# Rotary sine products and a bias-and-mask sum on GpSimd, with ScalarE copying swapped half tiles, in a kernel of four attentions and four feed-forward blocks

## The chip, the cores and the metric

The kernel runs on one core of one Trainium2 chip. The metric is the device time of one execution in microseconds (us): before the change, a median of 3104.46 over three runs (3103.13 to 3104.69). A core has five instruction queues, and each one starts its instructions in a fixed order: TensorE (PE in the profile; its weight loads are shown apart as PEld), VectorE (DVE), ScalarE (ACT), GpSimd (POOL) and SyncE (SP), which here only issues transfers. TensorE writes into PSUM; every operand of GpSimd in this kernel lies in SBUF.

## The reference, cut to what matters

The input x is 8 sequences of 128 tokens of 512 numbers. Eight blocks follow one another, each adding f(layernorm(x)) to x. The two that the change touches are the first and the third attention, with 32 heads of 128 numbers each. `ctx` is a second input that gives keys and values.

```python
# first attention: a bias per head, a mask per sequence
score = jnp.einsum('bhqd,bhkd->bhqk', h_q, h_k)
score = score + position_bias[None]
score = jnp.where(m, score, -jnp.inf)
score = jax.nn.softmax(score, axis=-1)
score = jnp.where(m, score, 0.0)
attn = jnp.einsum('bhqk,bkhd->bqhd', score, h_v)

# third attention: rotary embedding; 8 key heads for 32 query heads
def _rotate_half(x):
    x1, x2 = (x[..., :x.shape[-1] // 2], x[..., x.shape[-1] // 2:])
    return jnp.concatenate([-x2, x1], axis=-1)
q = q * cos + _rotate_half(q) * sin
k = k * cos + _rotate_half(k) * sin
scores = jnp.einsum('bhqd,bhkd->bhqk', q, k) / jnp.sqrt(jnp.float32(D))
```

The other six blocks are a mixture of low-rank experts, a small attention with heads of 8 numbers, an int8 feed-forward block, a feed-forward block whose weights are rounded to a 16-value code (NF4), a fourth attention with normed queries and keys, and a block of gated experts.

## The kernel before

**Units.** A unit is one head of one half of the batch (four sequences, `hf` 0 or 1). The first attention has 64 units (`Unit0`), the third 64 (`Unit2`), and one loop in the program runs over all 128 of them. A group `g` is four heads; in the third attention the four share one key head. While the loop is at unit u, it projects the query (and the key) of unit u+3, takes scores and softmax of unit u+2, and multiplies the probabilities of unit u with its values. After the last head of a group come the four output projections (`output`, in `out_proj`, L218), for the third attention spread over the first two units of the next group.

**One unit of the first attention.** `project_k` and `project_q` (L337 to L352) project 128 features for 512 tokens into a PSUM bank (`project`, L237), and ScalarE copies them out. `score` (L361) gets the scores of four sequences into one bank (L265). VectorE adds the bias while it reads the bank (L363), adds the mask `neg0` (bf16; -3e38 where masked) to the result (L364), takes the row maximum (L256); ScalarE exponentiates (L213); VectorE divides (L259, L366, L367). The probabilities are turned by VectorE in 32 x 32 blocks (L277) and by transfers through a scratch tensor, and `weigh` multiplies them with the values (L288), copied out by ScalarE (L290).

**One unit of the third attention.** The same, without bias, and with `rope` (L651) between projection and scores: VectorE multiplies the PSUM bank by the cosines (L653), then the lower 64 rows by their sines into the upper half of a tile `r` and the reverse (L655, L656), and GpSimd adds both (L657). The table `cs` holds cosines and, beside them, sines for the rows 0 to 63 and negated sines for the rows 64 to 127. Features lie on the partitions, so the swap of halves is a move across partitions. The query is the weight operand of the scores (`lhsT=self.q`), the key the moving one. ScalarE scales the probabilities (L694).

**Buffers.** The pools have a fixed number of buffers by name. PSUM has eight banks: two for projections and outputs of this stream (`mm`), one each for turns, scores and pv, and three for the side work. Score tiles (`s`) have two buffers, shared by name with `o` of the fourth attention (L1020); `r` and the bias share two (`rot`); queries and keys have three each, `o` six (`tile_of`).

**Side work and order.** The blocks between the first and third attention of a half run beside the units of the other stage, in slots: `slot()` is called after each piece of a unit and emits what a table has for it (`short_stages`), and with it a share of the NF4 rounding on VectorE (L725, L726), which is ordered behind the last score read (`mark`) by `issue_after`. So, beside the first half of the third attention's units, the second half of the batch goes through the experts, the small attention (L502 to L563) and the int8 block. `inv_sqrt` (L157, L159), the root of every norm, runs on GpSimd, and VectorE waits for it (L183). The row gathers for the rotary tables (L641) are issued by GpSimd too. The framework orders the instructions of each engine as they become ready by its own estimate, with the program's order as priority, gives buffers, and adds the waits; the order of an engine is then fixed.

**Start.** The first norms and context loads of sequences 0 and 1 use the main stream's wide tiles `h` (two buffers) and `sq` (one), those of 2 and 3 the side stream's.

Of the kernel before, what the change touches and what calls it, by code (L numbers as in the profile page):

```python
# [11 lines left out]
F32 = mybir.dt.float32  # L12
# [6 lines left out]
ALU = mybir.AluOpType  # L19
# [4 lines left out]
P = 128  # L24
# [4 lines left out]
HALF = 4  # L29
# [33 lines left out]
def kernel(ctx: ExitStack, tc: tile.TileContext, a, out):  # L63
    nc = tc.nc
    V, S, G, T = nc.vector, nc.scalar, nc.gpsimd, nc.tensor

    def pool(name, bufs, **kw):
        return ctx.enter_context(tc.tile_pool(name=name, bufs=bufs, **kw))
# [9 lines left out]
    ap_ = pool("att", 2)  # L78
    dram = pool("scratch", 1, space=DRAM)

    class Stream:
# [27 lines left out]
        def wide(self, tag, shape=(P, 512), bufs=2):  # L109
            return self.sb.tile(list(shape), F32, tag=tag, name=tag, bufs=bufs)  # L110
# [8 lines left out]
    def weight(src, shape=(P, 512), queue=nc.sync):  # L119
        w = wtile(shape)  # L120
        queue.dma_start(w, src)
        return w

    def by_chunk(src, queue=nc.sync):

        return [weight(src[:, c, :], queue=queue) for c in range(4)]

    def of_head(src, h):

        return weight(src[:, :, h * P:(h + 1) * P], (P, DC, P))  # L130

    def along(v, n):

        return v.unsqueeze(2).to_broadcast([v.shape[0], v.shape[1], n])

    def times(v, n):

        return v.unsqueeze(1).to_broadcast([v.shape[0], n, v.shape[1]])
# [24 lines left out]
    for b in range(B):  # L163
        t = keep.tile([P, D], F32, name=f"x{b}")
# [4 lines left out]
    neg0 = keep.tile([P, B, P], BF16, name="neg0")  # L169
# [63 lines left out]
    def project(st, w, xT):  # L233

        mm = st.mm()
        for c in range(DC):
            T.matmul(mm, lhsT=w[:, c, :], rhs=xT[:, c, :], start=c == 0, stop=c == DC - 1)  # L237
        return mm

    def tile_of(name, bufs, shape=(P, 512)):  # L240
        return qkv.tile(list(shape), F32, tag=name, name=name, bufs=bufs)
# [6 lines left out]
    class Unit:  # L248
# [17 lines left out]
            return sc  # L266

        def score_tile(self):
            return ap_.tile([P, HALF, P], F32, tag="s", name="s")

        def turn(self):
            pt = p_transposed(self.st, self.p, S)
# [12 lines left out]
        def weigh(self):  # L285
            pv = self.st.pv()
            for i in range(HALF):
                T.matmul(pv[:, i, :], lhsT=self.values(i), rhs=self.pt[i], start=True, stop=True)  # L288
            o = tile_of("o", 6, (P, HALF, P))
            S.copy(o, pv)  # L290
            self.group.o.append(o)
# [5 lines left out]
    mark = [None]  # L297
# [38 lines left out]
    class Unit0(Unit):  # L336
# [8 lines left out]
        def project_q(self):  # L345
            st, g, grp = self.st, self.g, self.group
            self.q = tile_of("q", 3)
            S.copy(self.q, project(st, of_head(a["l0_wq"][g], self.h), xT0[self.hf]))
            if self.h == 0:
                self.load_values()  # L350
            if self.h == 3:
                grp.wo = by_chunk(a["l0_wo"][g])  # L352
# [6 lines left out]
            return [self.project_k, self.project_q]  # L359

        def score(self):  # L361
            s = self.score_tile()
            mark[0] = V.tensor_add(s, self.scores(self.k), times(self.group.bias[:, self.h, :], HALF))  # L363
            V.tensor_add(s, s, neg0[:, self.hf * HALF:(self.hf + 1) * HALF, :])  # L364
            self.softmax(s)
            V.tensor_mul(self.su, self.su, anyv[:, self.hf * HALF:(self.hf + 1) * HALF])  # L366
            V.tensor_mul(s, s, along(self.su, P))  # L367
# [283 lines left out]
    def rope(dst, mm, t):  # L651

        V.tensor_mul(dst, mm, t[:, 0, :])  # L653
        r = ap_.tile([P, 512], F32, tag="rot", name="rot")
        V.tensor_mul(r[0:64, :], mm[64:128, :], t[64:128, 1, :])  # L655
        V.tensor_mul(r[64:128, :], mm[0:64, :], t[0:64, 1, :])  # L656
        G.tensor_add(dst, dst, r)  # L657

    class Unit2(Unit):
        def project_k(self):  # L660
            st, g, grp = self.st, self.g, self.group
            w = grp.w = [weight(a["l2_wkv"][g][:, 2 * j:2 * j + 2, :], (P, 2, 2 * P)) for j in range(2)]
            grp.ctx = ctxT[:, :, self.hf * 512:(self.hf + 1) * 512]
            mm = st.mm()
            for c in range(DC):
                T.matmul(mm, lhsT=w[c // 2][:, c % 2, 0:P], rhs=grp.ctx[:, c, :], start=c == 0, stop=c == DC - 1)  # L666
            grp.k = tile_of("k", 3)
            rope(grp.k, mm, cs[self.hf])
# [11 lines left out]
        def project_q(self):  # L680
            self.q = tile_of("q", 3)
            rope(self.q, project(self.st, of_head(a["l2_wq"][self.g], self.h), xT2[self.hf]), cs[self.hf])
            if self.h == 3:
                self.group.wo = by_chunk(a["l2_wo"][self.g])
# [215 lines left out]
    class L3:  # L900
# [115 lines left out]
        def weigh(self, it):  # L1016
            pv = self.st.pv()
            for j in range(2):
                T.matmul(pv, lhsT=it.v[:, j, :], rhs=it.pts[j], start=j == 0, stop=j == 1)  # L1019
            it.o = ap_.tile([P, 4, P], F32, tag="s", name="o")  # L1020
            if it.blocks:
                S.copy(it.o.rearrange("p h (a j) -> p a h j", j=32), pv.rearrange("p a (h j) -> p a h j", j=32))
            else:
                S.copy(it.o, pv)
# [68 lines left out]
    with ExitStack() as early:  # L1093
        def sub_pool(name, bufs, **kw):
            return early.enter_context(tc.tile_pool(name=name, bufs=bufs, **kw))

        ps = sub_pool("ps", 1, space=PSUM)
        qkv = sub_pool("qkv", 5)
        nfp = sub_pool("nf4", 2)
        main = Stream("m", sub_pool("main", 2), ps, {"mm": ("mm", 2), "tp": ("tp", 1), "sc": ("sc", 1), "pv": ("pv", 1)})  # L1100
        side = Stream("s", sub_pool("side", 2), ps, {k: ("side", 3) for k in ("mm", "tp", "sc", "pv", "po")})


# [112 lines left out]
        for kind in (Unit0, Unit2):  # L1216
            for hf in range(2):
                for g in range(NG):
                    grp = Group()
# [69 lines left out]
    ps = ctx.enter_context(tc.tile_pool(name="ps2", bufs=1, space=PSUM))  # L1289
# [160 lines left out]
def build(arrays):  # L1450
    import concourse.bacc as bacc

    nc = bacc.Bacc("TRN2", target_bir_lowering=False, num_devices=1)
    aps = {
        n: nc.dram_tensor(f"in_{n}", v.shape, mybir.dt.from_np(v.dtype), kind="ExternalInput").ap()
        for n, v in arrays.items()
    }
    out = nc.dram_tensor("out_0", (B, P, D), F32, kind="ExternalOutput").ap()
    with tile.TileContext(nc) as tc:
        kernel(tc, aps, out)  # L1460
    return nc
# [9 lines left out]
```

## Time and profile before

| what | value |
|---|---|
| runs | 3103.13, 3104.46, 3104.69 us |
| profiled execution: its own time / the span from its first to its last instruction | 3106.4 / 3104.6 us |
| granted TensorE clock, mean | 0.998 |
| first attention, 0 to 1103 us: busy PE / DVE / ACT / POOL | 1093.9 / 812.2 / 363.6 / 47.7 us |
| third attention, 1103 to 1893 us: busy PE / DVE / ACT / POOL | 773.5 / 647.8 / 334.3 / 127.6 us |
| NF4 feed-forward, 1893 to 2133 us: busy PE / DVE / ACT / POOL | 238.7 / 48.3 / 19.5 / 5.5 us |
| fourth attention and last block, 2133 to 3104.6 us: busy PE / DVE / ACT / POOL | 965.7 / 507.5 / 368.8 / 114.8 us |

How to read a profile here: a row of a group has the source line, the engine, the operation, the tiles it writes and reads, the shapes and the count; then the busy time in us and the mean of one in ns; then how long the engine sat idle just before and which instruction ended that. A line number can be a helper's. In the list of waits, a row is the waiting instruction, what it waited for, and total us, times and longest. In the timeline a row is start, length, engine, line, operation; the bracket is the idle time before it. The end of a matmul is modelled, and matmuls overlap one another, so that TensorE counts as busy as long as the next one starts soon enough.

### The profile page before, as it was taken

The page shows a single profiled execution, that of the slowest core. Times are in us where ns is not written, and L with a number is a line of the kernel's source. Part 1 is how long each engine was busy: PE and PEld are TensorE (multiplying, and loading weights), DVE is VectorE, ACT ScalarE, POOL GpSimd, SP SyncE. Part 2 cuts the span into 40 slices and gives each one's busy share as a digit, 9 for nine tenths or more (in the row PEclk, how much of TensorE's full clock was granted, in tenths as well). Part 3 has the DMA queues.
Part 4 walks back from the last instruction along what each step waited for, and adds up shares of the span by engine and source line. Part 5 has one row for each costly group of instructions (what it writes and reads, how often), then busy time and mean ns, then how long its engine had stood idle before and what let it go on. Part 6 is the DMA issues. An engine that isn't in the chain of part 4 may idle for free.

```text
span 3104.6 us, 34843 instructions
## 1 busy us (share of the span) xinstructions
PE 3071.9 (99%) x10976; PEld 1694.2 (55%) x10980; DVE 2015.8 (65%) x4209; ACT 1086.1 (35%) x3410; POOL 295.5 (10%) x315
## 2 busy tenths in 40 slices
PE   9999999999999999999999999999999999999999
PEld 4554555545554565555555554445665665555564
DVE  5877787667767766888989983113555555555544
ACT  3222222235543233655333332002434433333332
POOL 2000000000001021111111110001111111111110
PEclk9999999999999999999999999999999999999999
DMA  6434343333334432323444342223655655555540
GB/s 216 124 113 126 117 126 116 102 103 97 102 95 118 150 119 80 102 82 113 123 140 128 119 124 84 77 69 103 181 178 165 187 180 174 180 172 167 174 132 14
DMA packets 414807, 393.83 MB, mean 127 GB/s; under 512 B 37600, under 2 KB 312736, under 8 KB 414112
## 3 DMA queue, kind: packets, MB, share of 16 engines
q1 hardware_dynamic: 391200, 348.60, 36.6%
q10 hardware_dynamic: 23040, 41.95, 4.4%
q8 instruction: 89, 1.46, 0.2%
q0 software_dynamic: 384, 1.05, 0.1%
q14 instruction: 94, 0.77, 0.1%
HBM read 291.92 MB, written 99.55 MB: 126 GB/s over the span
## 4 chain that ended last, share of the span: by engine, by line
PE 84%; DVE 11%; ACT 2%; DMA 2%; issue 1%; POOL 0%; SPq 0%; ACTq 0%; POOLq 0%; DVEq 0%
PE mm L237 17%; PE mm L218 12%; PE po L218 7%; PE tp L921 7%; PE mm L376 7%; PE mm L944 7%; PE mm L879 5%; PE pv L1019 4%; PE sc L996 3%; PE pv L288 2%; PE mm L888 2%; PE sc L265 2%; ACT s L213 1%; DVE dq L726 1%; DVE rot L656 1%; PE mm L666 1%
## 5 line engine op out<-in xcount | busy, mean ns | idle before, releaser
L237 PE MATMUL mm<-xT,w 128*128 128x512 f32 x1024 | 464.4, 595 | 2.1 <-DVE rot L656 2.1
L218 PE MATMUL mm<-w,o 128*128 128x512 f32 x1024 | 464.0, 597 | 1.6 <-ACT o L290 1.5
L726 DVE TENSOR_TENSOR dq<-dq,ind 128x512 f32<-128x512 f32 (+2 forms) x476 | 326.8, 687 | 9.8
L237 PEld LDWEIGHTS mm<-xT,w 128*128 128x128 f32 x1024 | 188.9, 190 | 218.6 <-issue 208.6
L218 PEld LDWEIGHTS mm<-w,o 128*128 128x128 f32 x1024 | 188.5, 191 | 214.3 <-issue 199.9
L213 ACT ACTIVATE s<-s,nm 128x128 f32<-128x128 f32 x512 | 199.0, 390 | 190.2 <-DVE nm L256 179.1
L944 PE MATMUL mm<-w,xT 128*128 128x512 f32 x512 | 233.9, 592 | 0.0
L218 PE MATMUL po<-w,o 128*128 128x512 f32 x512 | 233.2, 594 | 0.0
L237 PE MATMUL mm<-ctxT,w 128*128 128x512 f32 x512 | 230.7, 593 | 1.1 <-ACT ctxT L1235 0.8
L376 PE MATMUL mm<-w,ctxT 128*128 128x512 f32 x512 | 230.4, 593 | 0.0
L725 DVE TENSOR_SCALAR ind<-nw 128x512 f32<-128x512 f32 (+2 forms) x476 | 210.5, 442 | 5.8
L213 ACT ACTIVATE p<-sc,nm,rq 128x256 f32<-128x256 f32 x256 | 141.1, 562 | 113.6 <-DVE nm L1001 109.9
L159 POOL TENSOR_TENSOR rs<-rs,mhalf 128x1 f32<-128x1 f32 x64 | 41.2, 645 | 1248.5 <-DVE rs L180 757.7
L265 PEld LDWEIGHTS sc<-k,q 128*128 128x128 f32 x1024 | 131.8, 192 | 49.5 <-issue 39.9
L219 DVE TENSOR_TENSOR x<-x,mm 128x512 f32<-128x512 f32 x128 | 87.0, 679 | 110.3 <-PE mm L218 110.0
L290 ACT COPY o<-pv 128x512 f32<-128x512 f32 x128 | 74.3, 581 | 237.6 <-PE pv L288 237.6
L218 PEld LDWEIGHTS po<-w,o 128*128 128x128 f32 x512 | 96.3, 190 | 110.6 <-issue 103.3
L879 PE MATMUL mm<-xT,w 128*128 128x512 f32 (+1 forms) x352 | 152.5, 592 | 0.8 <-DVE x L219 0.8
L376 PEld LDWEIGHTS mm<-w,ctxT 128*128 128x128 f32 x512 | 94.3, 190 | 106.2 <-issue 106.2
L1000 DVE TENSOR_REDUCE nm<-sc 128x2 f32<-128x512 f32 x128 | 85.3, 674 | 102.7 <-PE sc L996 102.5
L237 PEld LDWEIGHTS mm<-ctxT,w 128*128 128x128 f32 x512 | 93.2, 190 | 99.3 <-issue 96.8
L944 PEld LDWEIGHTS mm<-w,xT 128*128 128x128 f32 x512 | 97.0, 190 | 89.5 <-issue 84.9
(244 smaller groups left out, 4716.5 us busy)
## 6 DMA issues: line engine op xcount, KB each, us to landing
w<-in_l_wq SPq DMA_DIRECT2D x128, 256.0 KB
w<-in_l_wo SPq DMA_DIRECT2D x128, 256.0 KB
far<-tb SPq DMA_DIRECT2D x125, 256.0 KB
pt<-far SPq DMA_DIRECT2D x500, 64.0 KB
far<-tb SPq DMA_DIRECT2D x60, 512.0 KB
pt<-far SPq DMA_DIRECT2D x240, 128.0 KB
far<-tb SPq DMA_DIRECT2D x63, 384.0 KB
pt<-far SPq DMA_DIRECT2D x252, 96.0 KB
```

The source lines that it names most:

```text
L213: S.activation(dst(h), src(h), AF.Exp, bias=negm[:, h:h + 1], scale=by, accum_out=su[:, h:h + 1])
L218: T.matmul(mm, lhsT=o(h), rhs=wo[h], start=h == 0, stop=h == 3)
L237: T.matmul(mm, lhsT=w[:, c, :], rhs=xT[:, c, :], start=c == 0, stop=c == DC - 1)
L265: T.matmul(sc[:, i, :], lhsT=self.q[:, i * P:(i + 1) * P], rhs=k[:, i * P:(i + 1) * P], start=True, stop=True)
L376: T.matmul(mm, lhsT=ctxT[:, c, toks(self.hf * HALF + i)], rhs=grp.wv[c], start=c == 0, stop=c == DC - 1)
L725: V.tensor_scalar(iv, w, bound, step, cmp, ALU.mult)
L726: V.tensor_add(dst, dst, iv)
L879: T.matmul(mm[:n, :], lhsT=w[c][:, j * P:j * P + n], rhs=xT[:, c, :], start=c == 0, stop=c == DC - 1)
L921: T.matmul(it.kv[:, s, :], lhsT=lhsT, rhs=it.wkv[c // 2][:, c % 2, :], start=c == 0, stop=c == DC - 1)
L944: T.matmul(mq, lhsT=self.xT[it.hf][:, c, cols(it.b)], rhs=it.wq[c], start=c == 0, stop=c == DC - 1)
L996: T.matmul(sc[:, i, :], lhsT=it.qT[2 * j + i], rhs=it.kT, start=True, stop=True)
L1019: T.matmul(pv, lhsT=it.v[:, j, :], rhs=it.pts[j], start=j == 0, stop=j == 1)
```

## The change

In the third attention, `rope` leaves the cosine product on VectorE. ScalarE copies the two halves of the PSUM bank, swapped, into `r`; GpSimd multiplies `r` by the sine table in place, and subtracts it from the cosine product (subtracts, since each row now meets the sine of its own half, of the other sign).

In the first attention, GpSimd adds bias and mask into the score tile when the query is projected, one loop step before the scores; VectorE then makes one addition, of the scores in PSUM and that tile.

Score tiles get three buffers, and with them `o` of the fourth attention. The main stream's `h` and `sq`, used at the start, take buffers of the name "o" (six) in place of tiles of their own.

```diff
--- before.py
+++ after.py
@@ -266,7 +266,7 @@
             return sc
 
         def score_tile(self):
-            return ap_.tile([P, HALF, P], F32, tag="s", name="s")
+            return ap_.tile([P, HALF, P], F32, tag="s", name="s", bufs=3)
 
         def turn(self):
             pt = p_transposed(self.st, self.p, S)
@@ -346,6 +346,9 @@
             st, g, grp = self.st, self.g, self.group
             self.q = tile_of("q", 3)
             S.copy(self.q, project(st, of_head(a["l0_wq"][g], self.h), xT0[self.hf]))
+
+            self.masked = self.score_tile()
+            G.tensor_add(self.masked, times(grp.bias[:, self.h, :], HALF), neg0[:, self.hf * HALF:(self.hf + 1) * HALF, :])
             if self.h == 0:
                 self.load_values()
             if self.h == 3:
@@ -359,9 +362,8 @@
             return [self.project_k, self.project_q]
 
         def score(self):
-            s = self.score_tile()
-            mark[0] = V.tensor_add(s, self.scores(self.k), times(self.group.bias[:, self.h, :], HALF))
-            V.tensor_add(s, s, neg0[:, self.hf * HALF:(self.hf + 1) * HALF, :])
+            s = self.masked
+            mark[0] = V.tensor_add(s, self.scores(self.k), s)
             self.softmax(s)
             V.tensor_mul(self.su, self.su, anyv[:, self.hf * HALF:(self.hf + 1) * HALF])
             V.tensor_mul(s, s, along(self.su, P))
@@ -652,9 +654,11 @@
 
         V.tensor_mul(dst, mm, t[:, 0, :])
         r = ap_.tile([P, 512], F32, tag="rot", name="rot")
-        V.tensor_mul(r[0:64, :], mm[64:128, :], t[64:128, 1, :])
-        V.tensor_mul(r[64:128, :], mm[0:64, :], t[0:64, 1, :])
-        G.tensor_add(dst, dst, r)
+        S.copy(r[0:64, :], mm[64:128, :])
+        S.copy(r[64:128, :], mm[0:64, :])
+
+        G.tensor_mul(r, r, t[:, 1, :])
+        G.tensor_tensor(dst, dst, r, ALU.subtract)
 
     class Unit2(Unit):
         def project_k(self):
@@ -1017,7 +1021,7 @@
             pv = self.st.pv()
             for j in range(2):
                 T.matmul(pv, lhsT=it.v[:, j, :], rhs=it.pts[j], start=j == 0, stop=j == 1)
-            it.o = ap_.tile([P, 4, P], F32, tag="s", name="o")
+            it.o = ap_.tile([P, 4, P], F32, tag="s", name="o", bufs=3)
             if it.blocks:
                 S.copy(it.o.rearrange("p h (a j) -> p a h j", j=32), pv.rearrange("p a (h j) -> p a h j", j=32))
             else:
@@ -1097,7 +1101,14 @@
         ps = sub_pool("ps", 1, space=PSUM)
         qkv = sub_pool("qkv", 5)
         nfp = sub_pool("nf4", 2)
-        main = Stream("m", sub_pool("main", 2), ps, {"mm": ("mm", 2), "tp": ("tp", 1), "sc": ("sc", 1), "pv": ("pv", 1)})
+
+        class Main(Stream):
+
+
+            def wide(self, tag, shape=(P, 512), bufs=2):
+                return tile_of("o", 6, shape) if tag in ("h", "sq") else super().wide(tag, shape, bufs)
+
+        main = Main("m", sub_pool("main", 2), ps, {"mm": ("mm", 2), "tp": ("tp", 1), "sc": ("sc", 1), "pv": ("pv", 1)})
         side = Stream("s", sub_pool("side", 2), ps, {k: ("side", 3) for k in ("mm", "tp", "sc", "pv", "po")})
 
 
```

## The prediction

> **What bounds the kernel now.** The page comes first: one engine is full, and VectorE is full only in part of the span.
>
> ```profile
> span 3104.6 us, 34843 instructions
> PE 3071.9 (99%) x10976; PEld 1694.2 (55%) x10980; DVE 2015.8 (65%) x4209; ACT 1086.1 (35%) x3410; POOL 295.5 (10%) x315
> DVE  5877787667767766888989983113555555555544
> ```
>
> TensorE idles 3104.6 - 3071.9 = 32.7 us. That is all that any gain can come from. The table of busy time by stretch says where it lies (columns: stretch, length, then busy us of PE, PEld, DVE, ACT, POOL).
>
> ```profile
> 100.00:200.00 100.00, 100.00 (x329) 51.84 (x328) 83.20 (x165) 24.96 (x71) 3.12 (x4) 1.00 0.41 123
> 800.00:900.00 100.00, 100.00 (x449) 52.37 (x448) 75.63 (x146) 53.74 (x184) 1.26 (x2) 1.00 0.30 92
> 1400.00:1500.00 100.00, 95.94 (x497) 56.09 (x497) 84.49 (x165) 50.76 (x169) 17.69 (x15) 1.00 0.35 108
> 1700.00:1800.00 100.00, 99.36 (x411) 58.66 (x409) 94.40 (x166) 35.17 (x129) 15.53 (x11) 1.00 0.40 124
> ```
>
> The first attention (to 1103) has no TensorE idle time between 100 and 900, with VectorE near 80%. The third (1103 to 1893) idles 790.0 - 773.5 = 16.5 us, half of the whole; VectorE reaches 94% there. TensorE's own waits name the releasers:
>
> ```profile
> PE mm L237 <- DVE rot L656: 2.1, 6, 0.4
> ...
> PE tp L454 <- DVE hw L452: 1.9, 1, 1.9
> PE tp L596 <- DVE q L591: 1.6, 1, 1.6
> ```
>
> With the smaller ones of that stage (L521 1.0, L443 1.0, L513 0.9, L219 0.7, L534 0.6, L813 0.5), VectorE ends 2.1 + 8.2 = 10.3 us of them. L656 is the rotation's last product: it frees the PSUM bank that a projection needs.
>
> **The rows that price the change.**
>
> ```profile
> L655 DVE TENSOR_TENSOR rot<-mm,cs 64x512 f32<-64x512 f32 x80 | 55.4, 693 | 1.5
> L364 DVE TENSOR_TENSOR s<-s,neg 128x512 f32<-128x512 f32 x64 | 44.2, 690 | 0.1
> L657 POOL TENSOR_TENSOR q<-q,rot 128x512 f32<-128x512 f32 x64 | 84.9, 1326 | 416.8 <-DVE rot L656 390.7 <-PE pv L288 6.4 <-PE sc L265 6.0
> L421 ACT COPY ha<-mm 128x128 f32<-128x128 f32 x8 | 2.1, 262 | 7.0 <-DVE lg L420 7.0
> ```
>
> **First attention: nothing.** It loses 64 x 0.69 = 44 us on VectorE (L364) and gains 64 GpSimd additions. None in the trace mixes f32 with bf16; the nearest row, L657, has 1.33, and L422 1.40: about 85 us. The addition takes no input from the projection. It needs the bias, the mask and a free score tile, whose last reader is the turn of three units ago, so it can run a unit ahead. TensorE, with no idle time, hides all of it and can gain nothing. Cover gone means the scores' evacuation waiting for GpSimd; GpSimd is nearly idle here (3.1 us in 100 to 200). On its queue the additions stand ahead of the norms' powers (L159) and of the eight row gathers (L641), for whose landing TensorE waits 4.1 us near 988: one addition late there costs 1.3, one VectorE product less gains 0.7. I take 0, ends -1 and +2. At the start the mask is ready at 22.0 and the first scores come at 45.4; three additions need 4 us. The start's norm tiles in "o" and the third buffer of "s" remove waits that TensorE doesn't have (the fourth attention's "o" releases none of its waits): 0. No DMA is added or moved.
>
> **Third attention, engine time.** Removed: 80 x (0.693 + 0.684) = 110 us of VectorE. Added: 160 ScalarE copies and 80 GpSimd products. No copy of 64 rows from PSUM is in the trace; the 64-row products at 0.69 cost as much as 128-row ones, so the nearest is L290, 128x512 from PSUM, 0.58: 93 us, taking ScalarE from 334 to 427 of 790. The product is an L657, 1.27 at its shortest: 102 to 106 us.
>
> Here a rule speaks against the change. The Trainium skill, "SBUF — State Buffer", section "Who interferes with whom", says that GpSimd and a VectorE instruction with two SBUF inputs, or in a two-port mode, exclude each other, the later one blocking until the first is done. If every one of the 144 new GpSimd instructions held VectorE for its whole length, 144 x 1.3 = 187 us would be lost against 154 removed. The trace has the effect (L725 below takes 1.08 where its mean is 0.44), but smaller: summing, over the 80 rotation additions, how far VectorE instructions that overlap one exceed their group's median gives 29 us, 0.36 for each. VectorE's other work there (PSUM reads, reductions, the 32x32 turns) isn't held. By the row, the third attention loses 80 x 0.36 = 29 more: VectorE 648 - 110 + 29 = 567 of 790. By the rule it would hardly be relieved. I take the row.
>
> **Third attention, the path to the scores.** This decides. The timeline of one group of heads, near 1690, engine by engine, put in order of time:
>
> ```profile
> 1688.17 0.69 DVE L653 TENSOR_TENSOR q<-mm,cs 128x512 f32<-128x512 f32 x1 [0.84 <-PE mm L237]
> ...
> 1690.44 1.27 POOL L657 TENSOR_TENSOR q<-q,rot 128x512 f32<-128x512 f32 x1 [10.81 <-DVE rot L656]
> 1690.91 1.08 DVE L725 TENSOR_SCALAR ind<-nw 128x512 f32<-128x512 f32 x1
> ...
> 1692.77 0.19 PEld L265 LDWEIGHTS sc<-k,q 128*128 128x128 f32 x1 [0.24 <-issue]
> ...
> 1693.89 0.68 DVE L653 TENSOR_TENSOR q<-mm,cs 128x512 f32<-128x512 f32 x1
> 1694.70 1.28 ACT L694 ACTIVATE s<-s,su 128x128 f32<-128x128 f32 x4 [0.43 <-DVE su L259]
> 1695.88 0.56 ACT L290 COPY o<-pv 128x512 f32<-128x512 f32 x1
> 1696.25 1.27 POOL L657 TENSOR_TENSOR q<-q,rot 128x512 f32<-128x512 f32 x1 [4.54 <-DVE rot L656]
> ...
> 1697.99 0.19 PEld L265 LDWEIGHTS sc<-k,q 128*128 128x128 f32 x1 [0.24 <-issue]
> ```
>
> The rotated query is the weight of its scores, loaded only one projection after its own. Now the path is three products and an addition, 1688.17 to 1691.71, 1.06 before the load. After it, the cosine product and ScalarE both read the same PSUM tile; where the kernel already has that pair (L420, L421) ScalarE waits for VectorE all seven times, so I put them in a row: 0.69 + 2 x 0.58 + 2 x 1.27 = 4.39, and 0.2 for four handovers (0.04 to 0.08 each): 4.6 in place of 3.54.
>
> Second head of a group: 1688.17 + 4.6 = 1692.77, just at its load. Any 0.3 of waiting shows; I take 0.2. Third head: VectorE, with two products less ahead, can take the cosine product at about 1693.4, done 1694.1. ScalarE is then in the softmax of the head before; the score read moves from 1690.30 to about 1689.05, so the scaling L694 ends near 1694.7. Copies before the scaling: the path ends at 1698.0, in time. Behind it: copies to 1695.9, GpSimd to 1698.6, late by 0.6. Behind the copy L290 too: late by 1.6. I take 0.7, nearest the middle. (Lower end 0: at 1611.52 GpSimd ended just 0.05 before the scores' matmul and TensorE had no gap. Upper end 1.8 for both heads.) First and fourth heads have outputs between: 8.4 and 15 us to spare. So 0.9 for each group; nine groups from 1503 on: 8.1, ends 0 and 16. Before 1503 the small attention's matmuls lie between and the spare time is mostly 2 to 20 us; five early queries (1107 to 1173) have 0.1 to 1.7: 5 x 0.7 = 3.5, ends 0 and 8. **Cost 11.6.**
>
> A late load stops TensorE, hence the next projection. Behind waiting copies on ScalarE stand exponentials, scalings and the copy of pv; behind waiting products on GpSimd stand the powers of the norms, for which VectorE's L183 waits. Both delay the side work, which has slots of spare time: 0, upper end 5.
>
> **Gains.** L656's 2.1: a key's bank is freed after 0.69 + 1.16 = 1.85 instead of 2.05, and VectorE comes sooner: all of it. Of the other 8.2 most are chains of short dependent instructions, which a shorter queue helps little: a third, 3.0 (ends 0 and 8.2).
>
> **Sum** on the profiled execution: 11.6 - 2.1 - 3.0 = +6.5. That execution took 3106.4, of which 1.8 lie outside the span of 3104.6; the runs' median is 3104.46. The change is added to the median: **3111.0**. About 0.2% (6.2 us) is what a measurement of this kernel can tell from no change.
>
> **Rivals.**
> - Faster, 3097 (0.23): the instruction order puts the copies ahead of the scaling, so both paths end in time and only the gains stay, with most of VectorE's waits: -2.1 - 5.5. Place: the third head; it decides where ScalarE starts the copies within 0.1 us of the cosine product. For it: ScalarE is idle two thirds of the time there, VectorE at 94%. Against: its idle gaps beside the third head are 0.4 to 0.8 long, shorter than two copies.
> - They cancel, 3106 (0.16): lateness of 0.3 a group.
> - ScalarE's queue becomes the bound, 3128 (0.13): copies stand behind the exponentials as well, 1.8 for each group and more beside the small attention, where ScalarE has 50 to 59% already. Against: TensorE now waits under 2 us for ScalarE's exponentials and pt copies.
> - VectorE isn't relieved, 3117 (0.06): the lock takes the removed time back as the rule has it, so gains vanish and products come later.
>
> **How the numbers follow.** Forecast 0.42, of which 0.12 lies below 3110.7 and 0.30 above, own range 3107 to 3118. Faster by over 0.2%: 0.20 of the first rival. Within: 0.12 + 0.16 + 0.03 = 0.31. Slower: 0.30 + 0.13 + 0.06 = 0.49. The range, 3096 to 3128, leaves out half of the faster rival's far end and half of the ScalarE one.
>
> **What would show it.** Right: TensorE waits for GpSimd at L265, about 10 us in sum and 0.5 to 1 each, none for L656; first attention without idle time as now; VectorE about 81 us less in 1103 to 1893; ScalarE's copies at 0.58. Wrong: copies that start beside the cosine product, a GpSimd product well off 1.3 us, scores put behind other matmuls so that the load isn't late, or VectorE instructions stretched by more than 0.4 for each GpSimd one.

## The result, and the profile after

The changed kernel takes **3120.89 us** (3119.44 to 3123.88), the kernel before, run beside it, 3104.69 (3103.13 to 3108.45): a ratio of 1.005, with a 95% interval of 1.0039 to 1.006, or 16.2 us slower. 3111.0 was forecast, within a range of 3096 to 3128.

The page of the changed kernel begins as follows; the third line shows VectorE's busy share in 40 slices.

```profile
span 3119.1 us, 35219 instructions
PE 3075.0 (99%) x10976; PEld 1693.0 (54%) x10980; DVE 1925.2 (62%) x3985; ACT 1182.5 (38%) x3570; POOL 483.4 (15%) x459
DVE  5877777667766756777778873113555555555544
```

TensorE's idle time rose from 32.7 to 3119.1 - 3075.0 = 44.1 us, although VectorE has 90.6 us less to do (2015.8 - 1925.2). The busy time by stretch of the changed kernel (stretch, length, then busy us of PE, PEld, DVE, ACT, POOL, granted clock) says where:

```profile
100.00:200.00 100.00, 100.00 (x329) 51.82 (x328) 80.52 (x159) 26.06 (x74) 10.46 (x9) 1.00 0.41 123
800.00:900.00 100.00, 100.00 (x449) 52.37 (x448) 73.41 (x142) 54.50 (x187) 7.31 (x7) 1.00 0.30 92
1103.00:1893.00 790.00, 763.08 (x3357) 439.54 (x3358) 582.34 (x1035) 421.12 (x1370) 234.90 (x187) 1.00 0.37 111
1400.00:1500.00 100.00, 94.88 (x485) 54.76 (x486) 76.86 (x151) 60.65 (x187) 28.99 (x25) 0.99 0.36 116
1700.00:1800.00 100.00, 95.03 (x388) 55.37 (x388) 84.34 (x138) 48.96 (x153) 31.21 (x24) 1.00 0.37 114
```

The first attention stays full. The third has 790 - 763.08 = 26.9 us without TensorE work, where the same stretch of the kernel before has 16.5:

```profile
1103.00:1893.00 790.00, 773.54 (x3397) 447.72 (x3397) 647.80 (x1201) 334.26 (x1225) 127.63 (x107) 1.00 0.37 113
```

VectorE's relief there is 647.80 - 582.34 = 65 us. So TensorE idles more, though VectorE is less busy. The first matmuls of the groups of heads date the loss: the changed kernel is 2.4 us ahead at 1487, 3.7 behind one group later, and then loses 0.5 to 2.4 us in each, to 15 at the NF4 block. TensorE's waits in the changed kernel (us in total, times, longest):

```profile
PE sc L265 <- POOL q L661: 9.1, 10, 1.9
...
PE mm L237 <- ACT rot L658: 2.8, 6, 0.7
...
PE tp L190 <- DVE rs L180: 2.4, 1, 2.4
PE mm L670 <- DVE x L219: 2.1, 3, 1.0
```

L265 takes the scores, with the rotated query as their weight; L661 is GpSimd's subtraction, L657 and L658 are ScalarE's copies, L660 is GpSimd's product, L351 the addition of bias and mask. The changed kernel's groups of instructions (busy us, mean ns | idle time before them):

```profile
L660 POOL TENSOR_TENSOR rot<-rot,cs 128x512 f32<-128x512 f32 x80 | 106.7, 1334 | 523.9 <-ACT rot L658 511.3 <-DVE s L695 4.8 <-DVE nm L256 3.4
L351 POOL TENSOR_TENSOR s<-bias,neg 128x512 f32<-128x512 f32 x64 | 81.3, 1272 | 727.3 <-DVE tb L277 476.6 <-ACT pt L228 103.6 <-ACT v L380 51.2
...
L657 ACT COPY rot<-mm 64x512 f32<-64x512 f32 x80 | 46.6, 582 | 212.3 <-DVE q L655 146.6 <-DVE k L655 61.0 <-issue 2.5
L658 ACT COPY rot<-mm 64x512 f32<-64x512 f32 x80 | 46.2, 577 | 0.9
```

The durations are those forecast. What isn't is how VectorE fares beside GpSimd. The timeline of one third head in the changed kernel, engine by engine, put in order of time, with instructions left out in between:

```profile
1740.59 0.41 DVE L817 TENSOR_TENSOR nw<-dq,am 128x256 f32<-128x256 f32 x1
1741.19 1.27 POOL L660 TENSOR_TENSOR rot<-rot,cs 128x512 f32<-128x512 f32 x1 [9.14 <-ACT rot L658]
1741.52 1.22 DVE L817 TENSOR_TENSOR nw<-dq,am 128x256 f32<-128x256 f32 x1
1742.54 1.33 POOL L661 TENSOR_TENSOR q<-q,rot 128x512 f32<-128x512 f32 x1
1742.66 1.82 DVE L817 TENSOR_TENSOR nw<-nw,ri 128x256 f32<-128x256 f32 x2
1743.10 0.19 ACT L213 ACTIVATION_READ_ACCUMULATOR s<-s,nm 128x1 f32 x1
1744.41 0.17 DVE L259 RECIPROCAL su<-su 128x4 f32<-128x4 f32 x1
1744.60 1.28 ACT L698 ACTIVATE s<-s,su 128x128 f32<-128x128 f32 x4 [1.32 <-DVE su L259]
1745.91 0.58 ACT L657 COPY rot<-mm 64x512 f32<-64x512 f32 x1
1746.51 0.58 ACT L658 COPY rot<-mm 64x512 f32<-64x512 f32 x1
1747.16 1.51 POOL L660 TENSOR_TENSOR rot<-rot,cs 128x512 f32<-128x512 f32 x1 [3.30 <-ACT rot L658]
1748.75 1.33 POOL L661 TENSOR_TENSOR q<-q,rot 128x512 f32<-128x512 f32 x1
1750.13 1.16 PE L265 MATMUL sc<-k,q 128*128 128x128 f32 x8 [0.63 <-POOL q L661]
```

An L817 takes 0.41 us alone; beside GpSimd the same form takes 1.22, and a pair 1.82. Behind them in VectorE's queue stands the softmax's reciprocal L259, ready when the exponentials ended at 1743.29, done at 1744.58. ScalarE's scaling L698 waits for it, the copies of the next head stand behind the scaling, and TensorE waits 0.63 us at the end. Without the 1.1 us by which L259 is late, the scores would probably have been in time. This is a reading of one head; the experiments ask whether it holds for the whole.

### The profile page after: what moved, and what is told of

Its sections match the earlier page's. It is cut to its first block, busy times and chain, and to the rows that moved or that the text cites. A ratio compares the mean times of both kernels' runs of the same rounds, so it can differ in the third digit from the quotient of the medians.

```text
span 3119.1 us, 35219 instructions
## 1 busy us (share of the span) xinstructions
PE 3075.0 (99%) x10976; PEld 1693.0 (54%) x10980; DVE 1925.2 (62%) x3985; ACT 1182.5 (38%) x3570; POOL 483.4 (15%) x459
## 4 chain that ended last, share of the span: by engine, by line
PE 83%; issue 7%; DVE 4%; POOL 4%; DMA 1%; ACT 1%; SPq 0%; POOLq 0%; ACTq 0%; DVEq 0%
PE mm L237 16%; PE mm L218 10%; PE po L218 7%; PE tp L925 7%; PE mm L378 7%; PE mm L948 7%; PE mm L883 5%; PE pv L1023 4%; PE sc L1000 3%; PE sc L265 3%; PE mm L892 2%; PE pv L288 2%; POOL rot L660 2%; POOL q L661 1%; PE sc L534 1%
## 5 line engine op out<-in xcount | busy, mean ns | idle before, releaser
L730 DVE TENSOR_TENSOR dq<-dq,ind 128x512 f32<-128x512 f32 (+2 forms) x476 | 347.5, 730 | 9.8
L729 DVE TENSOR_SCALAR ind<-nw 128x512 f32<-128x512 f32 (+2 forms) x476 | 224.9, 472 | 6.1
L351 POOL TENSOR_TENSOR s<-bias,neg 128x512 f32<-128x512 f32 x64 | 81.3, 1272 | 727.3 <-DVE tb L277 476.6
L660 POOL TENSOR_TENSOR rot<-rot,cs 128x512 f32<-128x512 f32 x80 | 106.7, 1334 | 523.9 <-ACT rot L658 511.3
L265 PEld LDWEIGHTS sc<-k,q 128*128 128x128 f32 x1024 | 130.7, 192 | 60.3 <-issue 36.2
L265 PE MATMUL sc<-k,q 128*128 128x128 f32 x1024 | 138.4, 278 | 9.1 <-POOL q L661 9.1
```

What stands on the lines that cost most here:

```text
L265: T.matmul(sc[:, i, :], lhsT=self.q[:, i * P:(i + 1) * P], rhs=k[:, i * P:(i + 1) * P], start=True, stop=True)
L660: G.tensor_mul(r, r, t[:, 1, :])
L729: V.tensor_scalar(iv, w, bound, step, cmp, ALU.mult)
L730: V.tensor_add(dst, dst, iv)
```

## The experiments

**Two theories.** P is the forecast's: the path from a projection to its scores or to its free bank has become longer, and that alone costs the time. The other (L in the first expectations, H in the later ones) is that the longer path is only where it shows, and GpSimd's instructions cost the time by holding VectorE back. In what follows, "stretch" is counted from the trace as in the prediction: how far VectorE's instructions that overlap a long GpSimd instruction in the third attention exceed the median of their group, each VectorE instruction once. It is 29 us before (80 GpSimd instructions) and 73 after (160). VectorE's busy time in the stage agrees: 647.8, less the 110 of the two products, plus the 44 by which the stretch grew, is 582, and 582.34 was measured. The later expectations count an instruction that overlaps both the product and the subtraction twice (58 do), and so work with a growth of 76 us; that is too high.

**One part alone.** First the changed kernel with the old rotation, so the edits of the first attention and the buffers alone; then the kernel before with the new rotation, which is the same edit the other way round.

```diff
-        S.copy(r[0:64, :], mm[64:128, :])
-        S.copy(r[64:128, :], mm[0:64, :])
-        G.tensor_mul(r, r, t[:, 1, :])
-        G.tensor_tensor(dst, dst, r, ALU.subtract)
+        V.tensor_mul(r[0:64, :], mm[64:128, :], t[64:128, 1, :])
+        V.tensor_mul(r[64:128, :], mm[0:64, :], t[0:64, 1, :])
+        G.tensor_add(dst, dst, r)
```

> Only the first attention's part of the change (GpSimd adds bias and mask ahead; three score tiles; the start's tiles under the name o); the rotation is the one of before. Theory P (the rotated query reaches the scores' weight load too late): this part is free, 3104.7 us, within 2 either way, and TensorE has no idle time between 100 and 900 us. Theory L (GpSimd holds VectorE): at most 1 us of loss, since in the changed kernel the 64 additions stretched VectorE by 10 us in a stage where TensorE never idles. Theory F (the first attention's part is a cause): 3110 or more.

> Only the new rotation; first attention, score tiles (two) and start as before. P and L: all of the loss, 3119 to 3123 us. F: clearly less, under 3115. If the third score tile had helped the third attention, more than 3123.

The first part alone: 3103.66 us against 3104.94, ratio 0.9995 (0.9987 to 1.0004): nothing. The rotation alone: 3119.44, ratio 1.0046 (1.0032 to 1.0059): all of the loss.

**Copies ahead of the cosine product.**

```diff
-        V.tensor_mul(dst, mm, t[:, 0, :])
         r = ap_.tile([P, 512], F32, tag="rot", name="rot")
         S.copy(r[0:64, :], mm[64:128, :])
         S.copy(r[64:128, :], mm[0:64, :])
+        V.tensor_mul(dst, mm, t[:, 0, :])
```

> The changed kernel with the two ScalarE copies written ahead of VectorE's cosine product, so that the copies need not wait for it; all instructions the same in number. P: the path from projection to GpSimd's last instruction is 0.7 us shorter where ScalarE is free, TensorE's wait for GpSimd at the scores falls from 9.1 to under 4 us and the time to 3112 to 3117. L: GpSimd works as long as before, VectorE is held as much, 3119 to 3122.

3113.42 us, ratio 1.0029 (1.0018 to 1.0041): 7.5 less than after, inside P's span for the time and outside L's. TensorE's waits in this kernel:

```profile
PE sc L265 <- POOL q L660: 6.8, 10, 1.2
PE mm L237 <- DVE k L658: 6.6, 7, 1.7
```

The wait at the scores fell from 9.1 to 6.8 only, where P had under 4, and the one for the key's bank rose, since its last reader is now VectorE. The stretch fell as well, from 73 to 53 us, so the run doesn't part the two theories.

**The late scores put behind other matmuls.** The third head's scores move behind the first output projection.

```diff
-            if u + 2 < len(units):
-                units[u + 2].score()
...
+            later = isinstance(unit, Unit2) and unit.h == 0 and isinstance(units[u - 1], Unit2)
+            if not later:
+                scores()
             unit.weigh()
...
+            if later:
+                slot()
+                units[u - 1].output(0)
+                scores()
+                slot()
+                units[u - 1].output(1)
```

> The changed kernel with the third head's scores of each group written behind the first output projection of the step in place of ahead of it: 3.4 us more between that head's projection and its scores, nothing else moved by hand. P: TensorE's wait for GpSimd at the scores falls from 9.1 to 2 us or less and the time by 5 to 9 us, to 3112 to 3116. L: VectorE is held as much as in the changed kernel (GpSimd's instructions are the same), so 3119 to 3122.

3118.95 us, ratio 1.0046 (1.0033 to 1.006). Of TensorE's waits at L265 for GpSimd one of 0.3 us is left; the list begins now:

```profile
PE mm L237 <- ACT rot L658: 7.1, 6, 1.7
```

The largest wait was taken away and 2 of the 16 us came back; the rest turned up at the key's bank. The stretch stays (75 us). P in its plain form, that the late scores are the loss, falls.

**GpSimd's hold by itself.** The kernel before, with one more GpSimd product for each rotation, behind the addition, on a tile whose result nobody reads.

```diff
         G.tensor_add(dst, dst, r)
+        G.tensor_mul(r, r, t[:, 1, :])
```

> The kernel before, with one more GpSimd product behind each rotation's addition, whose result nobody reads: 80 instructions of about 1.3 us, off every path to scores, nothing taken from or added to VectorE and ScalarE. Theory H (GpSimd holds VectorE back; the lost time is side work that comes late): the stretch of VectorE instructions under GpSimd, 29 us before, grows by 0.4 to 0.9 for each of the 80, to 60 to 100 us, and the time by 6 to 16 us, to 3111 to 3121. Theory P (only the length of the path to scores and banks costs time): the path is untouched, so 3103 to 3107.

3129.59 us, ratio 1.0071 (1.0058 to 1.0085): 23 us for 80 instructions on no path, more than the whole change costs and 8 over what H expected. Its five executions lie apart, at 3123.3, 3123.9 and 3129.6 to 3130.8 us, with a granted clock of 0.995 to 0.997 where the kernel before had 0.996 to 0.998, so a part of the 23 may be the clock; the profiled one is the shortest, its span 3121.5 - 3104.6 = 16.9 us longer than before. The order of the instructions on TensorE, VectorE and ScalarE is the same as before, one by one. The stretch rose from 29 to 57 us, less than the 60 to 100 that H named. Its stage and its largest waits for VectorE:

```profile
1103.00:1893.00 790.00, 762.55 (x3345) 439.35 (x3346) 673.56 (x1195) 330.36 (x1210) 237.91 (x187) 0.99 0.36 111
```

```profile
PE mm L237 <- DVE rot L656: 3.9, 7, 1.4
...
PE mm L677 <- DVE x L219: 3.2, 5, 0.9
PE tp L454 <- DVE hw L452: 2.9, 1, 2.9
```

TensorE is idle 27.5 us in the stage, about as in the changed kernel, and no single wait stands out. Since the ends of matmuls are modelled, the waits can also be counted from their starts (how far a step from one matmul to the next exceeds the median of its form, where that is over 0.15 us): from 1096 to 1925, TensorE waits 29.4 us for VectorE where it waited 15.5 before.

The idle products could have cost time in two other ways: by holding back the powers of the norms, which stand in GpSimd's queue too, or by keeping one of the two buffers `rot` from the next rotation. Both would be waits of VectorE for GpSimd, and the only such row in the stage is, in both kernels:

```profile
DVE h L183 <- POOL rs L159: 3.3, 7, 0.7
```

**The product back on VectorE.** GpSimd keeps the subtraction alone, so it has 80 instructions as before.

```diff
-        G.tensor_mul(r, r, t[:, 1, :])
+        V.tensor_mul(r, r, t[:, 1, :])
```

> The changed kernel with the rotation's sine product on VectorE, from the copied tile in SBUF; GpSimd has the subtraction alone, as many instructions as before. VectorE still loses 80 x (1.38 - 0.7) = 54 us of products. Path: 0.69 + 2 x 0.58 + 0.70 + 1.33 + handovers = 4.1 us against 3.5 before and 4.6 to 5.6 after. Theory H: the stretch under GpSimd goes back to about 30 us, and with VectorE relieved the time falls to 3100 to 3106. Theory P: half of the added path is left, with ScalarE's copies behind the scaling: 3109 to 3114, and TensorE's wait at the scores L265 some 4 to 6 us.

3113.23 us, ratio 1.0023 (1.0013 to 1.0032): 7.7 less than after, though VectorE has 56 us more to do. P's span for the time holds, though not its 4 to 6 us at the scores; H expected a larger gain. The stretch is 35 us. The rest stands in TensorE's waits:

```profile
PE mm L237 <- ACT rot L658: 8.1, 7, 1.5
...
PE sc L265 <- POOL q L661: 3.0, 5, 1.3
```

ScalarE brings the copies late here too, and now VectorE stands in its own queue behind them: 24.7 us of idle time before the product L660.

**Some heads only.** New rotation for the first and fourth query head of a group, or for the second and third; keys and the others as before.

```diff
-            rope(self.q, project(...), cs[self.hf])
+            (rope_apart if self.h in (0, 3) else rope)(self.q, project(...), cs[self.hf])
```

> The changed rotation only for the first and fourth query head of each group, which have 8 and 15 us to spare; keys and the two middle heads as in the kernel before. Theory P: no wait for GpSimd at L265, keys' banks free as before, 3103 to 3106. Theory H: 32 of the 80 rotations have a second GpSimd instruction, so 0.4 of the 16 us is left: 3109 to 3113, and the stretch under GpSimd is some 29 + 0.4 x 76 = 60 us.

> The counterpart: the changed rotation only for the second and third query head, which have no time to spare; keys and the other two as in the kernel before. Theory P: the wait at L265 for GpSimd stays at 7 to 10 us, and the time is 3113 to 3119. Theory H: as many rotations changed as with the first and fourth head, so the same stretch (about 60 us) and 3109 to 3113.

First and fourth: 3117.83 us, ratio 1.0035 (1.0021 to 1.0049). Second and third: 3115.23, ratio 1.0027 (1.0017 to 1.0038). The heads with 8 and 15 us to spare cost at least as much as those with none. TensorE's first wait in the kernel with heads one and four:

```profile
PE mm L237 <- DVE rot L658: 9.5, 7, 1.6
```

L658 is there the last product of an old rotation, as a rule the key's. It is what it was before, where the same wait was 2.1 us; VectorE comes to it later. With heads one and four P misses by 12 us and H by 5; with two and three P's numbers hold (L265 waits 8.8 us), and H is 2 us low. Neither theory has both, and 32 rotations cost more than half of what 80 do: the cost isn't in proportion to their number.

**Copies first, and less on GpSimd.**

Against the run with the copies ahead of the cosine product, the sine product on VectorE:

```diff
-        G.tensor_mul(r, r, t[:, 1, :])
+        V.tensor_mul(r, r, t[:, 1, :])
```

> The changed kernel with ScalarE's copies ahead of the cosine product and the sine product on VectorE; GpSimd has the subtraction alone. 80 GpSimd instructions fewer than after, and both middle heads' copies no longer wait for the cosine product. Theory H (GpSimd's hold on VectorE makes most of the loss, ScalarE's late copies the rest): both causes are lessened, so 3103 to 3107, stretch under GpSimd about 30 us. Theory S (what is left of the loss with the product on VectorE, 7 us, comes from VectorE's queue standing behind copies that ScalarE brings late): the two products now both wait for the copies, so 3110 to 3115 as with the product on VectorE alone, with VectorE idle for the copies 25 us or more.

And against that, the subtraction too:

```diff
-        G.tensor_tensor(dst, dst, r, ALU.subtract)
+        V.tensor_tensor(dst, dst, r, ALU.subtract)
```

> The same, with the subtraction on VectorE too: no GpSimd instruction is left in the rotation. VectorE in 1103 to 1893 against before: 648 - 110 - 29 + 2 x 80 x 0.69 = 620 us. Theory H: no hold is left and VectorE has 28 us less than before, path 1.16 + 3 x 0.69 + handovers = 3.4 us: 3099 to 3105. Theory S: VectorE still stands behind late copies, 3108 to 3114.

With the subtraction on GpSimd 3105.27 us, ratio 0.9998 (0.999 to 1.0006), as H has it, with a stretch of 33 us; with none of the rotation on GpSimd **3093.66**, ratio 0.996 (0.9947 to 0.9974), 5 us below what H expected. S, a ScalarE queue that stays late, falls for both. Against the run with the product on VectorE and the copies behind the cosine product, the first of the two differs in the order of the copies alone: the stretch is the same (35 and 33), and 8.0 us are gone. By the starts of the matmuls, TensorE's wait for ScalarE falls there from 11.5 to 2.5 us, while the one for GpSimd rises from 4.3 to 7.8. So late copies are a cause of their own, which the hold doesn't need.

**The kernel before with its addition on VectorE.** One word differs.

```diff
-        G.tensor_add(dst, dst, r)
+        V.tensor_add(dst, dst, r)
```

> The kernel before with the rotation's addition on VectorE in place of GpSimd; nothing else. The hold of 29 us goes, 80 x 0.69 = 55 us of work comes: VectorE 648 - 29 + 55 = 674 of 790. Path to the scores 0.6 us shorter. Theory H (what counts is VectorE's time, held or worked): 26 us more of it against the 76 us that cost 16 to 22, so +3 to +8, 3108 to 3113. Theory P (length of the path): 3102 to 3106.

**3093.50 us**, ratio 0.996 (0.9946 to 0.9973): both expectations were wrong, H even in sign. A held microsecond costs more than a worked one.

**The idle product on top of that.** Path and VectorE's work as in the run just told, and again a GpSimd product for each rotation that nobody reads.

```diff
-        G.tensor_add(dst, dst, r)
+        V.tensor_add(dst, dst, r)
+        G.tensor_mul(r, r, t[:, 1, :])
```

> The kernel before with the rotation's addition on VectorE (3093.5 us) and one idle GpSimd product behind each rotation, whose result nobody reads: as many GpSimd instructions as in the kernel before, but on no path. Path to scores and VectorE's own instructions are those of the kernel at 3093.5. Theory H (each 80 long GpSimd instructions in the third attention cost 12 to 23 us, by the time they hold single VectorE instructions back): 3105 to 3116, with a stretch of 25 to 60 us. Theory P (the addition on VectorE gained by the shorter path to scores): 3091 to 3096.

3117.86 us, ratio 1.0041 (1.0027 to 1.0054): 24 us above the run without it, somewhat more than H expected and far from P. The stretch is 35 us, where the run without it has none. The two have the same order on TensorE, VectorE and ScalarE. The stage of the kernel with the addition on VectorE:

```profile
1103.00:1893.00 790.00, 780.72 (x3420) 452.26 (x3421) 669.20 (x1298) 334.56 (x1225) 22.37 (x31) 1.00 0.37 115
```

and with the idle product added to it:

```profile
1103.00:1893.00 790.00, 765.06 (x3369) 441.34 (x3369) 697.72 (x1280) 330.30 (x1210) 128.46 (x107) 1.00 0.35 111
```

The first idles 9.3 us on TensorE with VectorE busy 669, the second 24.9. By the starts of the matmuls, TensorE waits 8.5 us for VectorE in the first and 28.5 in the second. The largest of these in the second is for the score bank, which VectorE is late to read; in the first the same wait is 0.3 us:

```profile
PE sc L265 <- DVE s L692: 5.0, 6, 1.5
```

So the shorter path isn't what gained; the missing GpSimd instructions are.

The run also prices worked time. It has as many long GpSimd instructions as the kernel before (80) and nearly the same stretch (35 and 29), and VectorE has the additions besides, 80 x 0.69 = 55 us: 13.0 us more than the kernel before, beside which it ran at 3104.82. So VectorE's work isn't free either.

**All forms of the rotation side by side.** They differ in single steps, so pairs of rows price a step (the kernel before, run beside each, had medians of 3104.7 to 3106.1):

| swap of halves | sine product | sum | long GpSimd instr. | us |
|---|---|---|---|---|
| VectorE's two products | same | VectorE | 0 | 3093.50 |
| ScalarE, ahead of cosine product | VectorE | VectorE | 0 | 3093.66 |
| VectorE's two products | same | GpSimd (before) | 80 | 3104.69 |
| ScalarE, ahead | VectorE | GpSimd | 80 | 3105.27 |
| ScalarE, behind | VectorE | GpSimd | 80 | 3113.23 |
| ScalarE, ahead | GpSimd | GpSimd | 160 | 3113.42 |
| ScalarE, behind | GpSimd | GpSimd (after) | 160 | 3120.89 |

- One 128x512 operation for each rotation moved from VectorE to GpSimd: +11.2 (row 1 to 3), +11.6 (2 to 4), +8.2 (4 to 6), +7.7 (5 to 7).
- ScalarE's copies behind the cosine product and not ahead of it: +8.0 (4 to 5), +7.5 (6 to 7).
- The swap on ScalarE in place of VectorE's two products: +0.2 (1 to 2), although VectorE then has 669 - 609 = 60 us less in the stage. This is a sum of two things that no run parts, VectorE's relief and what the swap on ScalarE costs: VectorE waits 18.0 us for the copies there. Its stage in row 2:

```profile
1103.00:1893.00 790.00, 781.93 (x3439) 452.15 (x3440) 608.64 (x1218) 426.08 (x1385) 20.84 (x30) 1.00 0.37 115
```

The framework's order differs a little between the rows (in these pairs, 53 to 279 of TensorE's 10980 weight loads stand elsewhere), and the rows were not all measured beside one another, so a single pair carries some of that; that the pairs agree speaks for the step itself. Rows 2 and 4 to 7 have the first attention's edits too, which were shown to cost nothing.

## Why the prediction was right, and where it was wrong

Slower, and inside the range: 16.2 us for a forecast of 6.5. That the range held is in part luck: the largest term, late scores, turned out not to be what costs the time. From before to after the table has one product onto GpSimd (about 8), the copies behind the cosine product (about 8), and the swap on ScalarE together with VectorE's relief (0).

- **First attention, 0: right.** 3103.66 against 3104.94, no idle TensorE time from 100 to 200 and 800 to 900. VectorE loses 44 us of additions there and its busy time falls by 29 (812.2 to 783.3); some 10 of the difference are stretch under the 64 additions, about 0.15 us for each.
- **Engine time: copies and product right** (0.58 and 1.33 measured). VectorE's relief was put at 81 us and is 65, the difference being stretch.
- **The hold by the row, 0.36 us for each GpSimd instruction: the step that failed, twice.** In size: the stretch grew by 44 us where 29 was forecast, 0.55 for each new product, 0.46 for each of the 160 instructions, over the 0.4 that was named as a sign of being wrong. And in what it costs: the forecast set stretch against removed work, as if both were VectorE's time, and called the difference relief. The runs part them: 80 idle products, with a stretch of 28 and 35 us, cost 23 and 24 us of the program, 0.3 us each, while 55 us more work on VectorE beside the same number of GpSimd instructions cost 13. The rule of the Trainium skill that the forecast weighed and set aside ("SBUF — State Buffer", "Who interferes with whom": the later one waits for the whole instruction) fits by kind: beside a GpSimd instruction the changed kernel's row maxima and score reads (93 of them) took their usual time within 0.02 us on average, while the additions L730, with two inputs in SBUF, took 0.63 more. Applied to every GpSimd instruction, as the upper case of the forecast did, it overstates the stretch, 0.15 to 0.55 us measured of 1.3; but its warning was nearer to the time than the row was. Another page says as much: "Perfetto Trace Analysis", section "Optimizing Scalar/DVE Operations", notes that moving operations between these two engines might not help. Four pairs of runs here say -8 to -12 us for 80 operations moved back to VectorE.
- **Path to the scores, 4.6 us and a cost of 11.6: right in the wait, wrong in what it costs.** The wait at L265 is 9.1 in ten, 0.2 to 1.9 each, where "about 10 us" was named. The second head's path took 4.6 to 5.0, the third's mostly 5.2 to 5.6, since its copies stood behind the scaling L698, the middle case. But putting the third scores later took that wait away and gave back 1.9 us. What the order of the copies costs is 7.5 to 8.0, and where TensorE doesn't meet it at the scores, it meets it at the key's bank, which the forecast had freed sooner. Two of the five early queries waited, 2.2 us where 3.5 was put, and nothing of it is left in the time: the changed kernel is ahead at 1487.
- **Norm powers behind GpSimd's queue, 0 with an upper end of 5: one case.** At 1493.91 a norm's power became ready behind the key's L660 and L661 (1493.87 to 1496.81); L183 waited, and TensorE idled 2.4 us. That is inside the upper end.
- **Gains, 5.1: none.** L656's 2.1 became L658's 2.8: the bank is now freed by ScalarE, and both engines come late. The other waits for VectorE remained: by the starts of the matmuls, all waits for VectorE are 15.5 us before and 13.9 after, and those for ScalarE rose from 6.4 to 9.0.
- **Rivals.** The faster one had the copies ahead of the scaling decide. No run shows that order: also where they are written ahead of the cosine product, the third head's copies mostly stand behind the scaling, and that kernel still lost 8.7 us. "VectorE isn't relieved", given 0.06, named the cause of about half of the loss and put the time at 3117; its chance was too small. Its mechanism differs in one point: VectorE is relieved, in sum, and is late all the same. "ScalarE's queue becomes the bound" comes nearest to the other half, though it was the wait for the cosine product, and not exponentials ahead, that was priced.

**What stays open** is why a held microsecond costs so much more than a worked one: by the runs above 23 us of time for 28 of stretch and 24 for 35, so 0.7 to 0.8 for each (0.6 by the profiled execution of the first), against 13 for 55 of work, 0.24 (estimates, the last from a kernel whose path to the scores is also a little shorter). The 12 us that the addition on VectorE gained are then the 24 of the 80 GpSimd instructions less the price of the work. Nor does the stretch price a step by itself: the product on GpSimd adds 38 us of stretch with the copies behind the cosine product and 20 with them ahead, and costs 8 both times. The timeline shows holds in lumps of about 0.8 to 1 us, right behind a rotation, ahead of softmax steps and banks that others wait for. That the lumps are the reason is argued from it and wasn't tried.

## What to carry to other kernels

Work that is moved from VectorE to GpSimd can come back as holds of VectorE's other instructions: before moving it, add a GpSimd instruction whose result nobody reads and time that; here it cost 0.3 us of the program for each, and moving such work back was a gain that the kernel before still had, 12 us by one word. The first attention's additions, moved to GpSimd too, cost nothing, in a stage where TensorE hardly idles (1093.9 us busy of 1103). An engine's busy share says little of what its relief is worth: VectorE at 85% of the stage with hardly a GpSimd instruction beside it kept TensorE fuller than VectorE at 74% with it. And a wait that vanishes when its instruction is put elsewhere was the sign of a late engine, not the cost itself: look at what stands ahead of that engine's late instruction, and whether the time moves.

## What had not been expected of the hardware

The same GpSimd instruction form stretches VectorE very differently by what VectorE does meanwhile: about 0.15 us for each addition of the first attention, 0.36 before in the third, 0.46 for each of the 160 after, and 0.12 for the product when the cosine product stands right beside it (copies ahead). The stretch falls unevenly on single instructions: an addition L730, 0.69 us as a rule, took up to 1.65. ScalarE is untouched by it: the 648 activations of 128x128 from 1096 to 1925 take 252.5 us before, and 252.5 with the idle products.
